# Splitting the bias product of a windowed attention into two half-width products, and moving one expert's matmul

## The chip, the cores and the metric

The kernel runs on one core of a Trainium2 chip. The metric is the device time of one execution in microseconds; a kernel's time is the median of its runs. The core has five engines, each with its own instruction stream: TensorE (PE in the profile: matmuls into PSUM; its weight loads have a row of their own, PEld), VectorE (DVE), ScalarE (ACT), GpSimd (POOL) and SyncE (SP), which here only issues DMAs. The engines wait for one another through semaphores. All data are 32-bit floats.

## The reference, cut to what matters

The input `x` is (2, 128, 256, 256). One layer adds a windowed attention and then a mixture of experts, each on a normalised input.

```python
# attention (b, 128 channels, 256 x 256), 4 heads of 32, 8x8 windows of queries, 12x12 of keys
qkv  = einsum('bchw,oc->bohw', layernorm_c(x), W_qkv)
attn = einsum('bnd,bmd->bnm', q * SCALE, k)
attn = attn + rel_pos_emb(q, rel_height, rel_width) + FIXED_MASK   # -inf off every second row, column
attn = softmax(attn)                                              # over the keys of one query
out  = einsum('bnm,bmd->bnd', attn, v)
x    = x + einsum('bchw,oc->bohw', out, W_out)
# experts: 8 experts of 128 -> 128, the best 2 of a token, weighted
t = layernorm_t(tokens(x))
p = softmax(t @ router_w + router_b);  top_p, top_i = top_k(p, 2);  top_p /= sum(top_p)
x = x + sum_k top_p[k] * (t @ expert_w[top_i[k]] + expert_b[top_i[k]])
```

`rel_pos_emb` is the sum of two terms: the query times the row of `rel_height` that belongs to the vertical distance between query and key, and the same with `rel_width` and the horizontal distance. Because of the mask a query only meets keys at an odd distance class, so that pixels of one parity of row and column form an attention of their own. A number added to all logits of one query does not change its softmax.

## The kernel before

A strip is 8 image rows; it falls into 4 *planes* by parity, so there are 2 x 32 x 4 = 256 planes of 4 x 128 = 512 queries. The main loop takes one plane per *stage*. While the attention of plane `n` runs, the projections of plane `n + 1` (`ahead`) are made, and the experts work on 512 tokens of an earlier strip. Generators are advanced step by step, and the order in which the loop advances them is the order of the instructions on every engine.

The projections of a plane, with `mm_tile` taking the next of three PSUM buffers that go round:

```python
def mm_tile(name):
    return ps_mm.tile([P, 512], F32, tag="mm", name=name)          # pool ps_mm: bufs=3

def project(n, state):
    ...
    values(0)                    # pvv: four 128x128 products, copied to vv by ACT
    yield
    pu = mm_tile(f"pu{n}")       # the bias product: 9 + 9 distances for each of 4 heads
    nc.tensor.matmul(pu, lhsT=wrel, rhs=inner, start=True, stop=True)
    uT = work.tile([P, PR, 4, 32], F32, tag="uT", name=f"uT{n}", bufs=1)
    nc.vector.transpose(uT, pu.rearrange("p (a m s) -> p a s m", a=PR, s=4))
    state["shift"] = lambda: shift(uT, n, state)
    yield
    ...                          # pk: keys, copied to kcol by ACT
    yield
    pq = mm_tile(f"pq{n}")
    nc.tensor.matmul(pq, lhsT=wq, rhs=inner, start=True, stop=True)
    ...                          # copied to qs by ACT
    yield
    values(4)
    yield
```

`shift` lays the distances out for the keys (two copies) and transposes them into `au`, from which the next stage's `scores` begins: 16 products with constant `keys` as weights put the bias into `att`, and 64 small ones add q times k.

The main loop, cut to the order of what the change touches (`ex` is the set of experts under way, `nxt` the one after it, `new` the one whose gates are being fetched):

```python
for n in range(n_planes + 7):
    ...
    next(score, None)            # bias products, first half of the scores
    ...                          # route(...): the gates of an earlier 512 tokens, on DVE
    next(score, None)            # second half of the scores; exp on ACT
    next(ahead, None)            # pvv, first half
    nxt.fetch(7, nc.scalar)
    ...                          # spread(...): transpose of the gates (gT), DMA to DRAM and back
    next(ahead, None)            # pu, and the transpose uT on DVE
    if n + 1 < n_planes:
        states[n + 1]["shift"]() # DVE
    next(ahead, None)            # pk
    next(ahead, None)            # pq
    for e in (4, 6, 7, 5):
        ex.product(e)
    ...
    next(norm, None)             # squares on ACT
    next(attn, None)             # row sums and first half of exp(scores) times v
    nxt.means()                  # DVE
    ...                          # nxt.times(0..4, 6): six products with the gates on DVE
    ex.end()                     # DVE: adds the experts' sum
    next(attn, None)             # second half; DVE: transpose of the sums, reciprocal
    next(attn, None)             # DVE: o
    ex = nxt
    next(norm, None)             # plt: sums for the norms
    ...
    next(ahead, None)            # pvv, second half
    ex.product(0)
    made = next(norm, None)      # DVE and ACT: 1 / deviation
    ex.product(1)
    ex.product(2)
    ...                          # POOL: times(5), ln1, times(7), columns
    next(outp, None)             # po: output product
    ex.product(3)
    next(outp, None)             # DVE: adds po to x
    ...
```

One `ex.product(e)` is a 128x128 by 128x512 product into a PSUM buffer of its own (`acc`).

Of the kernel before, what the change touches and what calls it, by code (L numbers as in the profile page):

```python
# [11 lines left out]
F32 = mybir.dt.float32  # L12
AF = mybir.ActivationFunctionType
ALU = mybir.AluOpType
# [3 lines left out]
P = 128  # L18
HEADS, DH = 4, 32
# [3 lines left out]
NEG = -1e30  # L23
# [16 lines left out]

R = 8
KR, KC = 6, 10
NK = KR * KC
SLOT = 64
BLOCK, FIRST_LIMIT = 256, 95
NU = 9


@with_exitstack
def kernel(
# [31 lines left out]
    work = ctx.enter_context(tc.tile_pool(name="work", bufs=2))  # L84
# [10 lines left out]
    def ctile(shape, name):  # L95
        return const.tile(shape, F32, tag=name, name=name)
# [24 lines left out]
    wall = ctile([P, 4, P], "wall")  # L121
# [51 lines left out]
    relT = []  # L173
    for rname, rsb in zip(("relh", "relw"), relsb):
        pr = mm_tile(f"p_{rname}")
# [5 lines left out]
        relT.append(rT)  # L181
    mid = n_rel // 2
    lo = mid - 2 * (PR - 1)
    relbd = ctile([P, P], "relbd")
    nc.gpsimd.memset(relbd, 0.0)
    for h in range(HEADS):
        hp = slice(h * DH, (h + 1) * DH)
        for j in range(2):
            c0 = h * DH + NU * j
            nc.vector.tensor_copy(  # L190
                relbd[hp, c0 : c0 + NU], relT[j][hp, lo : lo + 2 * NU - 1 : 2]
            )
    wrel = ctile([P, P], "wrel")
    pr = mm_tile("p_wrel")
    nc.tensor.matmul(pr[:, :P], lhsT=wall[:, 0, :], rhs=relbd, start=True, stop=True)
    nc.vector.tensor_copy(wrel, pr[:, :P])

    xn, xcol, kcol = [], [], []
    for i in range(2):
# [8 lines left out]
        nc.gpsimd.memset(kcol[i][:, NP - 1, KC - 1 : NK : KC], 0.0)  # L208


    auT = []
    for i in range(2):
        auT.append(ctile([P, PR, 4, 32], f"auT{i}"))
        nc.gpsimd.memset(auT[i], 0.0)
        nc.gpsimd.memset(auT[i][:, :, :, KR + 6 : KR + 7], NEG)


    def rstd(p4, k0, k1, name):
# [123 lines left out]

    def shift(uT, n, state):

        for j in range(2):
            shifted = uT[:, :, :, NU * j + 3 : NU * j + 9]
            dims = [list(d) for d in shifted.ap]
            dims[1 + j][0] -= 1
            nc.vector.tensor_copy(
                auT[n % 2][:, :, :, 6 * j : 6 * j + 6],  # L350
                bass.AP(shifted.tensor, shifted.offset, dims),
            )
        au = work.tile([P, 2 * NP, PR, 4], F32, tag="au", name=f"au{n}")
        nc.vector.transpose(au.rearrange("p m a s -> p a s m"), auT[n % 2])  # L354
        state["au"] = au

    def project(n, state):

        i, pl = divmod(n, 4)
        xp = xn[i % 2][:, pl // 2, pl % 2]  # L360
        inner = xp[:, 1 : 1 + PR, 1 : PC + 1]
        xl, kk = xcol[pl], kcol[pl]

        vv = work.tile([P, HP, P], F32, tag="vv", name=f"vv{n}")

        def values(t0):
            pv = mm_tile(f"pvv{n}_{t0}")
            for t in range(4):
                nc.tensor.matmul(  # L369
                    pv[:, t * P : (t + 1) * P],  # L370
                    lhsT=xl[:, t0 + t].rearrange("p a k -> p (a k)"),
                    rhs=wv,
                    start=True,
                    stop=True,
                )
            nc.scalar.copy(vv[:, t0 : t0 + 4, :].rearrange("p t c -> p (t c)"), pv)  # L376

        values(0)
        yield

        pu = mm_tile(f"pu{n}")
        nc.tensor.matmul(pu, lhsT=wrel, rhs=inner, start=True, stop=True)  # L384
        uT = work.tile([P, PR, 4, 32], F32, tag="uT", name=f"uT{n}", bufs=1)
        nc.vector.transpose(uT, pu.rearrange("p (a m s) -> p a s m", a=PR, s=4))  # L386
        state["shift"] = lambda: shift(uT, n, state)
        yield

        rows = list(ln_rows(i))  # L390
        for part in (rows[-4:], rows[:-4]):
            if not part:
                continue
            pk = mm_tile(f"pk{n}_{part[0]}")
            m = len(part)
            nc.tensor.matmul(  # L396
                pk[:, : m * PC],
                lhsT=wk,
                rhs=xp[:, part[0] : part[0] + m, 1 : PC + 1],
                start=True,  # L400
                stop=True,
            )
# [33 lines left out]
    def scores(n, state):  # L436


        qs, kk, au = state["qs"], state["kk"], state["au"]
        turn = place(n // 4, 0) // 2  # L440
        att = ps_att.tile([P, 4, 512], F32, tag="att", name=f"att{n}")
        sc = att[:, :, 0:HQ]
        for w in range(2):
            for half in range(2):
                rows = slice(half * SLOT, (half + 1) * SLOT)
                for h in range(HEADS):
                    hp = slice(h * DH, (h + 1) * DH)
                    nc.tensor.matmul(
                        sc[rows, h].rearrange("p (t w z) -> p t w z", w=2, z=16)[:, :, w],
                        lhsT=keys[hp, turn, w],  # L450
                        rhs=au[hp, half * NP + w : (half + 1) * NP : 2].rearrange(
                            "p t a s -> p t (a s)"
                        ),
                        start=(w == 0),
                        stop=False,
                    )
        for t in range(HP):
            if t == HP // 2:
                yield
            for half in range(2):  # L460
                rows = slice(half * SLOT, (half + 1) * SLOT)
                m0 = 2 * (half * HP + t)
                for h in range(HEADS):
                    hp = slice(h * DH, (h + 1) * DH)
                    nc.tensor.matmul(  # L465
                        sc[rows, h, 32 * t : 32 * t + 32],
                        lhsT=kk[hp, half * HP + t, :],
                        rhs=qs[hp, m0 : m0 + 2].rearrange("p m a s -> p (m a s)"),
                        start=False,
                        stop=(t == HP - 1),  # L470
                    )
# [257 lines left out]
    n_planes = 4 * len(strips)  # L729
# [19 lines left out]
    states = {0: {}}  # L749
    for _ in project(0, states[0]):  # L750
        pass
    states[0]["shift"]()
    if n_planes > 1:
        columns(1)

# [17 lines left out]
    gated, ex, nxt = None, NoExperts(), NoExperts()  # L773
# [4 lines left out]
    with tc.manual_schedule(engines={ET.PE, ET.DVE, ET.Activation, ET.Pool, ET.SP}):  # L778
        for n in range(n_planes + 7):
            i, pl = divmod(n, 4)  # L780
            score, attn, outp, ahead, norm, rout = none, none, none, none, none, none
# [44 lines left out]
            next(attn, None)  # L826
            nxt.means()
            new.fetch_means()
# [12 lines left out]
            ex = nxt  # L841
# [84 lines left out]
```

The softmax here doesn't subtract the row's maximum and nothing guards it: scores larger than these inputs give would overflow.

## Time and profile before

| | |
|---|---|
| time, median of 3 | 4486.36 us (4485.98 to 4488.05) |
| span of the profiled execution | 4480.1 us |
| DVE busy | 3996.2 us (89%) |
| ACT busy | 1467.7 us (33%) |
| POOL busy | 1317.7 us (29%) |
| mean TensorE clock granted | 0.997 of full speed |
| DMA | 828.12 MB, 185 GB/s on average |

A busy time is the time in which an engine had at least one instruction under way. Matmuls overlap, so a record of a matmul lasts longer than the step to the next one: times per product are therefore read as differences between starts in the timeline. A 32-bit product of 128x512 leaves two records. The row of the engine that is nearly always busy, and the timeline of one stage, are shown in the prediction, where they are read.

In the timeline a line is: start in us, length in us, engine, line of the program, operation, output<-inputs, shape, number of records merged, and in brackets the idle time before it and who ended it.

### The profile page before, as it was taken

How to read it: one execution, taken by the hardware profiler on the slowest of the kernel's cores; microseconds unless marked ns; L12 is line 12 of the kernel's file. 1: busy time of each engine (PE TensorE's matmuls, PEld its weight loads, DVE VectorE, ACT ScalarE, POOL GpSimd, SP SyncE). 2: the span in 40 equal slices, each digit the busy share in tenths (PEclk: the TensorE clock that was granted, in tenths of full speed). 3: DMA queues.
4: the chain of work that ended last, by engine and by line, in shares of the span. 5: the costliest groups of instructions: out<-in, count | busy, mean ns of one | idle time of the engine just before them, and what ended most of it. 6: DMA issues, size and time to landing. Idle time of an engine off the chain costs nothing. (4 is left out here: it accounts for less than half of the span.)

```text
span 4480.1 us, 224632 instructions
## 1 busy us (share of the span) xinstructions
PE 4422.6 (99%) x96321; PEld 2683.3 (60%) x96321; DVE 3996.2 (89%) x11850; ACT 1467.7 (33%) x4022; POOL 1317.7 (29%) x1815
## 2 busy tenths in 40 slices
PE   7999999999999999999999999999999999999997
PEld 5666666666666666666666666666666666666653
DVE  5899999999899999998989999999999999989887
ACT  3333333333333333333333333333333333333321
POOL 1232323232323233232323232323232323232321
PEclk9999999999999999999999999999999999999999
DMA  2565666566656666666666566666665666566655
GB/s 83 174 191 185 192 185 192 186 191 185 193 184 192 185 191 187 189 188 188 189 187 189 187 190 185 193 183 193 184 193 185 192 185 192 186 191 186 190 164 186
DMA packets 519284, 828.12 MB, mean 185 GB/s; under 512 B 124186, under 2 KB 125850, under 8 KB 518298
## 3 DMA queue, kind: packets, MB, share of 16 engines
q1 hardware_dynamic: 517568, 813.46, 58.3%
q8 instruction: 769, 12.60, 1.1%
q14 instruction: 217, 1.78, 0.2%
q10 hardware_dynamic: 730, 0.29, 0.0%
HBM read 737.95 MB, written 75.56 MB: 182 GB/s over the span
## 5 line engine op out<-in xcount | busy, mean ns | idle before, releaser
L686 PE MATMUL acc<-xe,ew 128*128 128x512 f32 x4096 | 1889.0, 594 | 19.6 <-DVE gb L660 18.8
L686 PEld LDWEIGHTS acc<-xe,ew 128*128 128x128 f32 x4096 | 758.8, 190 | 885.7 <-issue 861.8
L677 DVE TENSOR_TENSOR xe<-xs,gb 128x512 f32<-128x512 f32 x1536 | 950.9, 687 | 10.2 <-PE acc L686 0.7
L681 POOL COPY last<-xe 128x1 f32<-128x1 f32 x256 | 47.9, 187 | 3060.8 <-DVE gb L660 3054.6
L376 ACT COPY vv<-pvv 128x512 f32<-128x512 f32 x512 | 299.8, 586 | 1395.7 <-PE pvv L369 1379.6
L677 POOL TENSOR_TENSOR xe<-xs,gb 128x512 f32<-128x512 f32 x512 | 650.8, 1272 | 5.9 <-PE att L496 2.5
L369 PE MATMUL pvv<-wt,xcol 128*128 128x128 f32 x4096 | 594.3, 288 | 2.5 <-POOL xcol L331 1.5
L369 PEld LDWEIGHTS pvv<-wt,xcol 128*128 128x128 f32 x4096 | 496.4, 191 | 64.8 <-issue 51.8
L272 POOL TENSOR_TENSOR xn<-xt,rb 128x512 f32<-128x512 f32 x249 | 375.0, 1506 | 66.5 <-DMA rb<-gd 55.9
L465 PE MATMUL att<-qs,kcol 32*64 32x32 f32 x32768 | 392.4, 226 | 0.8 <-issue 0.7
L465 PEld LDWEIGHTS att<-qs,kcol 32*64 32x64 f32 x32768 | 391.0, 130 | 1.0 <-issue 1.0
L496 PEld LDWEIGHTS att<-pT,vv 64*32 64x32 f32 x32768 | 348.0, 105 | 39.4 <-issue 2.5
L496 PE MATMUL att<-pT,vv 64*32 64x32 f32 x32768 | 343.2, 200 | 2.3 <-issue 2.3
L473 ACT ACTIVATE pT<-att 128x1024 f32<-128x1024 f32 x256 | 261.9, 1023 | 243.1 <-PE att L465 239.7
L548 ACT ACTIVATE sq<-xt 128x512 f32<-128x512 f32 x505 | 292.7, 631 | 0.0
L354 DVE STREAM_TRANSPOSE au<-auT 128x512 f32<-128x512 f32 x256 | 269.2, 1052 | 9.0
L524 PE MATMUL po<-o,wt 128*128 128x512 f32 x512 | 262.0, 593 | 6.1 <-DVE o L516 3.2
L384 PE MATMUL pu<-xn,wrel 128*128 128x512 f32 x512 | 262.5, 594 | 0.0
L407 ACT COPY kcol<-pk 128x560 f32<-128x560 f32 (+2 forms) x344 | 174.1, 506 | 268.2 <-PE pk L396 265.3
L418 PE MATMUL pq<-xn,wt 128*128 128x512 f32 x512 | 262.0, 593 | 0.0
L396 PE MATMUL pk<-xn,wt 128*128 128x512 f32 (+2 forms) x528 | 261.0, 578 | 0.0
L386 DVE STREAM_TRANSPOSE uT<-pu 128x512 f32<-128x512 f32 x256 | 182.8, 714 | 78.0 <-PE pu L384 77.0
(2697 smaller groups left out, 5243.8 us busy)
## 6 DMA issues: line engine op xcount, KB each, us to landing
gb<-gd SPq DMA_DIRECT2D x2048, 256.0 KB, 4.0
xt<-in_x_dram SPq DMA_DIRECT2D x256, 256.0 KB, 4.9
sb<-gd SPq DMA_DIRECT2D x256, 256.0 KB, 3.5
out_dram<-xt SPq DMA_DIRECT2D x256, 256.0 KB, 4.2
rb<-gd SPq DMA_DIRECT2D x249, 256.0 KB, 3.3
gd<-gT SPq DMA_DIRECT2D x516, 16.0 KB, 3.0
ew<-in_L_ffn_expert_w_dram SPq DMA_DIRECT2D x1, 512.0 KB, 5.0
eb<-in_L_ffn_expert_b_dram SPq DMA_DIRECT2D x1, 512.0 KB, 5.7
```

Source lines behind the costliest of these rows:

```text
L272: eng.tensor_tensor(xn[i % 2][:, :, :, k, 1 : PC + 1], ln1_src(i, k).rearrange("p (y j x) -> p y x j", y=2, x=2), rb.rearrange("p (y j x) ...
L354: nc.vector.transpose(au.rearrange("p m a s -> p a s m"), auT[n % 2])
L369: nc.tensor.matmul(pv[:, t * P : (t + 1) * P], lhsT=xl[:, t0 + t].rearrange("p a k -> p (a k)"), rhs=wv, start=True, stop=True,)
L376: nc.scalar.copy(vv[:, t0 : t0 + 4, :].rearrange("p t c -> p (t c)"), pv)
L384: nc.tensor.matmul(pu, lhsT=wrel, rhs=inner, start=True, stop=True)
L418: nc.tensor.matmul(pq, lhsT=wq, rhs=inner, start=True, stop=True)
L465: nc.tensor.matmul(sc[rows, h, 32 * t : 32 * t + 32], lhsT=kk[hp, half * HP + t, :], rhs=qs[hp, m0 : m0 + 2].rearrange("p m a s -> p (m a ...
L496: nc.tensor.matmul(av[hp, half, 32 * t : 32 * t + 32], lhsT=vv[rows, t, hp], rhs=pT[rows, h, 32 * t : 32 * t + 32], start=True, stop=True,)
L524: nc.tensor.matmul(po, lhsT=wo, rhs=state["o"].rearrange("p f z -> p (f z)"), start=True, stop=True)
L548: nc.scalar.activation(sq, src, AF.Square)
L677: eng.tensor_tensor(self.xe[e], self.xs, self.gb.pop(e), ALU.mult)
L686: nc.tensor.matmul(self.acc, lhsT=ew[:, e, :], rhs=self.xe.pop(e), start=(e == 0), stop=not self.xe)
```

## The change

Three things are done together.

1. The bias product is halved. The value for the last distance is subtracted from the other eight when the weights `relbd` are built, once, so that 8 + 8 columns (`NB = 16`) per head are left instead of 9 + 9, and 64 weight columns for the four heads. The plane's 512 queries are cut into two halves of 256; both use the same 64 columns, one writes PSUM partitions 0 to 63 and the other 64 to 127. `pu` and `uT` have half the columns. `shift` needs four copies and two clearings for the layout, and its last transpose writes a tile `both` of half the size. In it the two halves stand on different partitions than the bias products want them, so a new step `send` moves them into a permanent `au` with eight small DMAs of 16 partitions x 1 KB each, issued from ACT.
2. The bias product stands directly behind the scores, ahead of the first half of `pvv`, and with it takes its PSUM buffer first.
3. `ex.product(3)`, which followed the output product `po`, is issued at the start of the next stage's group behind `pq`, ahead of experts 4, 6, 7 and 5.

`FIRST_LIMIT` (where the instruction stream of a stage is aligned) goes from 95 to 99, for the four instructions that the second half product adds.

```diff
-BLOCK, FIRST_LIMIT = 256, 95
+BLOCK, FIRST_LIMIT = 256, 99
 NU = 9
+NB = 16
@@ weights of the bias product @@
-            nc.vector.tensor_copy(
-                relbd[hp, c0 : c0 + NU], relT[j][hp, lo : lo + 2 * NU - 1 : 2]
+            c0 = h * NB + (NU - 1) * j
+            last_d = lo + 2 * (NU - 1)
+            nc.vector.tensor_tensor(
+                relbd[hp, c0 : c0 + NU - 1],
+                relT[j][hp, lo : last_d - 1 : 2],
+                relT[j][hp, last_d : last_d + 1].broadcast_to([DH, NU - 1]),
+                ALU.subtract,
             )
@@ shift @@
-        for j in range(2):
-            shifted = uT[:, :, :, NU * j + 3 : NU * j + 9]
             ...
-        au = work.tile([P, 2 * NP, PR, 4], F32, tag="au", name=f"au{n}")
-        nc.vector.transpose(au.rearrange("p m a s -> p a s m"), auT[n % 2])
+        for up, (rows, start) in enumerate(((slice(0, 64), 3), (slice(64, P), 1))):
             ...                                  # one copy each, on 64 partitions
+        for h in range(2):
             ...                                  # one copy each
+        nc.vector.memset(to[0:64, 0, :, :, 5:6], 0.0)
+        nc.vector.memset(to[:, :, 0, :, 11:12], 0.0)
+        both = work.tile([P, 2 * NP, 8], F32, tag="both", name=f"both{n}")
+        nc.vector.transpose(
+            both.rearrange("p m (a s) -> p a s m", a=2), to.rearrange("p a s h k -> p a s (h k)")
+        )
+    def send(n, state):
+        both = state.pop("both")
+        for up in range(2):
+            for h in range(HEADS):
+                r = (up * HEADS + h) * NB
+                nc.scalar.dma_start(au[n % 2][h * DH : h * DH + NB, up], both[r : r + NB])
@@ project @@
-        values(0)
-        yield
         pu = mm_tile(f"pu{n}")
-        nc.tensor.matmul(pu, lhsT=wrel, rhs=inner, start=True, stop=True)
-        uT = work.tile([P, PR, 4, 32], F32, tag="uT", name=f"uT{n}", bufs=1)
-        nc.vector.transpose(uT, pu.rearrange("p (a m s) -> p a s m", a=PR, s=4))
+        for up in range(2):
+            nc.tensor.matmul(
+                pu[up * 64 : (up + 1) * 64, 0 : NQ // 2],
+                lhsT=wrel,
+                rhs=inner[:, 2 * up : 2 * up + 2],
+                start=True,
+                stop=True,
+            )
+        uT = work.tile([P, 2, 4, 32], F32, tag="uT", name=f"uT{n}", bufs=1)
+        nc.vector.transpose(uT, pu[:, 0 : NQ // 2].rearrange("p (a m s) -> p a s m", a=2, s=4))
         state["shift"] = lambda: shift(uT, n, state)
         yield
+        values(0)
+        yield
@@ main loop @@
             next(score, None)
-            next(ahead, None)
             nxt.fetch(7, nc.scalar)
             ...
                 states[n + 1]["shift"]()
             next(ahead, None)
             next(ahead, None)
-            for e in (4, 6, 7, 5):
+            next(ahead, None)
+            for e in (3, 4, 6, 7, 5):
                 ex.product(e)
             ...
             next(norm, None)
+            if n + 1 < n_planes:
+                send(n + 1, states[n + 1])
             next(attn, None)
             ...
             next(outp, None)
-            ex.product(3)
             next(outp, None)
```

More of the change, by code (lines that the diff above doesn't have):

```diff
@@ L183 @@
     lo = mid - 2 * (PR - 1)
-    relbd = ctile([P, P], "relbd")
+    relbd = ctile([P, HEADS * NB], "relbd")
     nc.gpsimd.memset(relbd, 0.0)
@@ L188 @@
         for j in range(2):
-            c0 = h * DH + NU * j
-            nc.vector.tensor_copy(
-                relbd[hp, c0 : c0 + NU], relT[j][hp, lo : lo + 2 * NU - 1 : 2]
+            c0 = h * NB + (NU - 1) * j
[5 more added lines that the diff above has]
+                ALU.subtract,
             )
-    wrel = ctile([P, P], "wrel")
+    wrel = ctile([P, HEADS * NB], "wrel")
     pr = mm_tile("p_wrel")
-    nc.tensor.matmul(pr[:, :P], lhsT=wall[:, 0, :], rhs=relbd, start=True, stop=True)
-    nc.vector.tensor_copy(wrel, pr[:, :P])
+    nc.tensor.matmul(
+        pr[:, : HEADS * NB], lhsT=wall[:, 0, :], rhs=relbd, start=True, stop=True
+    )
+    nc.vector.tensor_copy(wrel, pr[:, : HEADS * NB])
     xn, xcol, kcol = [], [], []
@@ L208 @@
         nc.gpsimd.memset(kcol[i][:, NP - 1, KC - 1 : NK : KC], 0.0)
-    auT = []
+    auT, au = [], []
     for i in range(2):
-        auT.append(ctile([P, PR, 4, 32], f"auT{i}"))
+        auT.append(ctile([P, 2, 4, 2, NB], f"auT{i}"))
         nc.gpsimd.memset(auT[i], 0.0)
-        nc.gpsimd.memset(auT[i][:, :, :, KR + 6 : KR + 7], NEG)
+        nc.gpsimd.memset(auT[i][:, :, :, :, KR + 6 : KR + 7], NEG)
+        au.append(ctile([P, 2, 2 * NP, 8], f"au{i}"))
+        nc.gpsimd.memset(au[i], 0.0)
     def rstd(p4, k0, k1, name):
@@ L343, in shift @@
     def shift(uT, n, state):
-        for j in range(2):
-            shifted = uT[:, :, :, NU * j + 3 : NU * j + 9]
-            dims = [list(d) for d in shifted.ap]
-            dims[1 + j][0] -= 1
+        to = auT[n % 2]
+        for up, (rows, start) in enumerate(((slice(0, 64), 3), (slice(64, P), 1))):
+            src = uT[rows, :, :, start : start + 6]
+            step, block = src.ap[1][0], src.ap[2][0]
+            dims = [list(src.ap[0]), [step - 1, 2], [block // 2, 8], [1, 6]]
             nc.vector.tensor_copy(
-                auT[n % 2][:, :, :, 6 * j : 6 * j + 6],
-                bass.AP(shifted.tensor, shifted.offset, dims),
-            )
-        au = work.tile([P, 2 * NP, PR, 4], F32, tag="au", name=f"au{n}")
-        nc.vector.transpose(au.rearrange("p m a s -> p a s m"), auT[n % 2])
-        state["au"] = au
+                to[rows, :, :, :, 0:6].rearrange("p a s h k -> p a (s h) k"),
+                bass.AP(src.tensor, src.offset, dims),
+            )
+        src = uT[:, :, :, NU + 2 : NU + 8]
+        step, block = src.ap[1][0], src.ap[2][0]
+        for h in range(2):
+            dims = [list(src.ap[0]), [step, 2], [block - 1, 4], [1, 6]]
+            nc.vector.tensor_copy(
+                to[:, :, :, h, 6:12], bass.AP(src.tensor, src.offset + h * NB, dims)
+            )
[4 more added lines that the diff above has]
+            both.rearrange("p m (a s) -> p a s m", a=2), to.rearrange("p a s h k -> p a s (h k)")
+        )
+        state["both"] = both
+    def send(n, state):
[4 more added lines that the diff above has]
+                nc.scalar.dma_start(au[n % 2][h * DH : h * DH + NB, up], both[r : r + NB])
     def project(n, state):
@@ L376, in values @@
             nc.scalar.copy(vv[:, t0 : t0 + 4, :].rearrange("p t c -> p (t c)"), pv)
-        values(0)
-        yield
-        pu = mm_tile(f"pu{n}")
-        nc.tensor.matmul(pu, lhsT=wrel, rhs=inner, start=True, stop=True)
-        uT = work.tile([P, PR, 4, 32], F32, tag="uT", name=f"uT{n}", bufs=1)
-        nc.vector.transpose(uT, pu.rearrange("p (a m s) -> p a s m", a=PR, s=4))
-        state["shift"] = lambda: shift(uT, n, state)
+        pu = mm_tile(f"pu{n}")
+        for up in range(2):
+            nc.tensor.matmul(
+                pu[up * 64 : (up + 1) * 64, 0 : NQ // 2],
[3 more added lines that the diff above has]
+                stop=True,
+            )
+        uT = work.tile([P, 2, 4, 32], F32, tag="uT", name=f"uT{n}", bufs=1)
+        nc.vector.transpose(uT, pu[:, 0 : NQ // 2].rearrange("p (a m s) -> p a s m", a=2, s=4))
+        state["shift"] = lambda: shift(uT, n, state)
+        yield
+        values(0)
         yield
@@ L436, in scores @@
     def scores(n, state):
-        qs, kk, au = state["qs"], state["kk"], state["au"]
+        qs, kk, bias = state["qs"], state["kk"], au[n % 2]
         turn = place(n // 4, 0) // 2
@@ L448, in scores @@
                     nc.tensor.matmul(
-                        sc[rows, h].rearrange("p (t w z) -> p t w z", w=2, z=16)[:, :, w],
+                        sc[rows, h].rearrange("p (t w a z) -> p t w a z", w=2, a=2, z=8)[:, :, w],
                         lhsT=keys[hp, turn, w],
-                        rhs=au[hp, half * NP + w : (half + 1) * NP : 2].rearrange(
-                            "p t a s -> p t (a s)"
+                        rhs=bias[hp, :, half * NP + w : (half + 1) * NP : 2].rearrange(
+                            "p a t z -> p t a z"
                         ),
@@ L752 @@
     states[0]["shift"]()
+    send(0, states[0])
     if n_planes > 1:
```

## The prediction

> **What bounds the kernel now.** I read the page's row of engines first, then the busy times over a long stretch, then the timeline of one stage on TensorE (PE) and the same on VectorE (DVE), and last the list of waits.
>
> ```profile
> PE 4422.6 (99%) x96321; PEld 2683.3 (60%) x96321; DVE 3996.2 (89%) x11850; ACT 1467.7 (33%) x4022; POOL 1317.7 (29%) x1815
> ```
>
> PE is busy all the time, and from 2000 to 2800 us it is busy for 799.99 of 800 us. DVE has 723.38 us there, 90%, so it is a close second. Busy alone does not prove that PE is the bound, since matmuls overlap; what proves it is that the starts on PE follow each other without a hole. One stage:
>
> ```profile
> 2001.45 0.69 PE L448 MATMUL att<-au,keys 32*64 32x128 f32 x32
> 2001.93 1.53 PE L465 MATMUL att<-qs,kcol 32*64 32x32 f32 x128
> 2003.39 1.16 PE L369 MATMUL pvv<-wt,xcol 128*128 128x128 f32 x8
> 2004.39 1.02 PE L384 MATMUL pu<-xn,wrel 128*128 128x512 f32 x2
> 2005.25 1.02 PE L396 MATMUL pk<-xn,wt 128*128 128x512 f32 x2
> 2006.11 1.02 PE L418 MATMUL pq<-xn,wt 128*128 128x512 f32 x2
> 2006.97 3.59 PE L686 MATMUL acc<-xe,ew 128*128 128x512 f32 x8
> 2010.49 0.66 PE L486 MATMUL att<-pT,ones 64*32 64x256 f32 x16
> ...
> 2012.22 0.43 PE L554 MATMUL plt<-xt,rw 128*32 128x128 f32 x8
> 2012.46 0.40 PE L554 MATMUL plt<-sq,rw 128*32 128x128 f32 x8
> 2012.68 0.40 PE L554 MATMUL plt<-xt,rw 128*32 128x128 f32 x8
> 2012.90 0.40 PE L554 MATMUL plt<-sq,rw 128*32 128x128 f32 x8
> 2013.23 1.16 PE L369 MATMUL pvv<-wt,xcol 128*128 128x128 f32 x8
> 2014.22 2.74 PE L686 MATMUL acc<-xe,ew 128*128 128x512 f32 x6
> 2016.80 1.02 PE L524 MATMUL po<-o,wt 128*128 128x512 f32 x2
> 2017.66 1.02 PE L686 MATMUL acc<-xe,ew 128*128 128x512 f32 x2
> 2018.61 0.69 PE L448 MATMUL att<-au,keys 32*64 32x128 f32 x32
> ```
>
> From bias product to bias product (L448) the stage takes 2018.61 - 2001.45 = 17.16 us. Every step between two starts can be read as a price: a product of 128x512 costs 0.86 (pu L384 to pk L396 to pq L418); four of them behind pq 3.52; bias 0.48; scores 1.46; half of pvv 1.00. The prices fill the stage, and nothing waits. DVE at the end of this stage and in the next:
>
> ```profile
> 2017.86 0.69 DVE L529 TENSOR_TENSOR xt<-po,xt 128x512 f32<-128x512 f32 x1
> ...
> 2022.09 0.24 DVE L625 STREAM_TRANSPOSE gT<-g 128x64 f32<-128x64 f32 x1
> 2022.61 0.72 DVE L386 STREAM_TRANSPOSE uT<-pu 128x512 f32<-128x512 f32 x1 [0.28 <-PE pu L384]
> 2023.36 0.33 DVE L349 COPY auT<-uT 128x96 f32<-128x96 f32 x2
> 2023.73 1.06 DVE L354 STREAM_TRANSPOSE au<-auT 128x512 f32<-128x512 f32 x1
> ```
>
> L529 adds the output product po to x. It starts 1.06 us after po's start on PE (2016.80), that is, as soon as po's records end (2016.80 + 1.02). Then DVE works without a pause through the routing until gT (L625) ends at 2022.33, and only there stands a hole: 0.28 us until pu is done. So DVE runs only just ahead of PE, and **its order is fixed: po's addition, routing, gT, uT**. The list of waits says the same for the whole run: uT waited for pu 186 times, 77.0 us in all, and the addition for po 11 times only, 3.5 us.
>
> **What the Trainium skill says.** (1) "Perfetto Trace Analysis", its opening note: matmul busy time is a bad measure, because matmuls are pipelined. The trace agrees (a record of 1.02 us with a step of 0.86), so I count in steps. (2) "TensorE: Matmul & The Clock Gate", "Part 3: Packing small matmuls": products in different column groups of the array run at the same time. The trace agrees: each of the four plt groups (L554) is four products with 32 weight columns each, on four column groups, and a group costs 0.22 us to 0.24 us, a quarter of the 1.00 us of the four full-width products of pvv. (3) The same page, Part 1: ScalarE and VectorE are strict FIFO, and on PE only weight loads are pulled ahead, matmuls stay in order. So a matmul that waits for a late DVE instruction holds up everything behind it. Nothing in this trace contradicts that; the wait itself is not yet in it.
>
> **The change part by part.**
>
> *The halved product.* It removes one product of 0.86. It adds two of 256 columns in two column groups; by (2) they should take the time of one, half of 0.86 = 0.43, plus one more change of the array's shape, for which the step from the last plt group to pvv, 0.33 instead of 0.22, gives 0.11. Sum 0.54, saving 0.32 per stage. If PE stayed dense, the stage would be 17.16 - 0.32 = **16.84 us**.
>
> *DVE's layout work.* Before: from uT to the next product L671 2024.63 - 2022.61 = 2.02 us. After: uT on half the columns, for which I interpolate between 128x128 (L563, 0.33) and 128x512 (0.72): 0.46; two copies of 96 elements at 0.17 per step, two of 48 at some 0.13, two clearings, and a last transpose of about half of L354's 1.05. Together about 1.7. DVE gains some 0.3 us; this is beside the path unless DVE is the bound.
>
> *The eight DMAs.* They leave ACT behind its squares. In the changed program some of them wait for slots that the gate transfers rb and sb have to free first. Before, sb landed some 8 us after gT's end (issued 4.56 after it, 3.5 to landing); with some 3 us more (the 16 KB gd writes take 3.0) the table is there 11 us after gT, while the next bias product comes about 13 us after it (see below). I take this as **hidden, with some 2 us to spare**.
>
> *Moving expert 3, and pu ahead of pvv.* This is what decides, and it removes no work. Two things happen.
>
> First, the buffers. mm tiles go round in three PSUM buffers. Before, the order was pvv, pu, pk, pq, so pq took the buffer of pvv, which ACT empties early (in the program before, pq waits for ACT's copy L376). After, the order is pu, pvv, pk, pq: **pq takes the buffer of pu and must wait until DVE has read it in uT**. In the changed program the wait in front of pq is indeed on DVE's uT.
>
> Second, the time of uT. It is tied to po by DVE's order: po's start + 1.06 to the addition, + 2022.33 - 2017.86 = 4.47 to the end of gT, + 0.46 for uT, + 0.04 to hand over (pu's end 2022.57 to uT's start 2022.61) = po + 6.03. And PE reaches pq sooner, since expert 3 no longer stands between po and the bias: 0.95 from po to the bias (the step 2017.66 to 2018.61, product and change of shape), 0.48, 1.46, 0.54 for pu, 1.00 for pvv, 0.86 for pk = po + 5.29. Before, PE got there at po + 0.86 + 0.95 + 4.66 = po + 6.47 and had no such wait. So **PE stands still for 0.74 us in front of pq**.
>
> The whole ring, as a check: from pq's start to po's start PE takes 2016.80 - 2006.11 = 10.69 before, and with expert 3 in it 11.55. Add po to pq, 6.03: **17.58 us per stage**, of which PE fills 16.84. PE must start again with a cold pipeline; some part of a weight load (0.19) may not be hidden: I add 0.06, 17.64. This is 0.48 more than before. Expert 3 is on the ring because it now stands between pq and po, while in its old place it lay beside the DVE's routing.
>
> Experts and projections are both there from stage 7 to 254, so 248 times: 248 x 0.48 = 119 us; the seven stages ahead of that gain some 2 us in all. 4486.4 + 119 - 2 = **about 4603 us**.
>
> **The rivals.**
>
> *PE stays dense (16.84).* Then 248 x 0.32 = 79 us are saved, 4405 us. For it: PE is the bound, and the halved product is cheaper by a mechanism that the trace shows. Against it: it needs uT to be done at po + 5.29, and DVE has 4.47 us of routing alone ahead of it. It would hold if DVE's order were another or the ring had a fourth buffer.
>
> *DVE becomes the bound.* In a stage of 17.16 DVE waits 0.28 for pu; without that and with 0.3 less layout work it needs about 16.6. Against it also: the sums' transpose L506 could start 6.7 after uT, but it needs the end of the product of weights and v, some 7.6 after uT's start, so DVE idles there. DVE counts as part of the ring, not as the bound.
>
> *The table comes late.* Then PE waits in front of the bias product. For it: a chain of three DMAs and an ACT engine that stands in line behind them. Against it: the 2 us to spare; and a delay of up to 0.74 would only take the place of the wait at pq. If it were 1 us late beyond that, the stage would be 18.6 us and the time near 4840.
>
> *GpSimd and DVE in each other's way.* Some DVE instructions are long because GpSimd is busy (L229 has a median near 0.82 but 0.16 in the first stages). With sT later, L229 may meet shorter GpSimd instructions. That would gain nothing, as DVE then waits for po.
>
> **Range and chances.** The ring is a sum of measured steps; open are uT's length, the restart, and the hand-over, together perhaps 0.15 to either side, so 0.32 to 0.63 per stage: 4566 to 4643, which I widen a little to **4560 to 4640**. 2% is 89.7 us, that is 0.36 per stage, at the lower end of this. Slower by over 2%: 0.79. Within 2%: 0.16, for a wait of half the size. Faster by over 2%: 0.05; even the dense rival gives only 1.8%.
>
> **What the changed profile would show.** Waits of PE (or PEld) at pq for DVE's uT, some 0.7 us each, near 180 us in all, and PE busy down to about 95%; no wait of uT for pu any more; DVE waiting some 0.9 us for PE at the transpose of the sums and some 0.7 us at po's addition; the pair of half products with a step near 0.5 us; no wait at the bias product; a stage of about 17.6 us. The prediction is wrong if pq starts without a hole (then 16.84 per stage and some 4405), if the half products do not overlap (this would shift the hole, not the stage), or if the bias product waits for a DMA.

## The result, and the profile after

The changed kernel takes **4683.0 us** (median of 4 runs, 4676.21 to 4694.24) against 4487.2 us before: ratio **1.0438, interval 1.0413 to 1.0463**. The prediction was 4603 us, with a range up to 4640. The direction was right, the size was not: 196 us were lost instead of 117.

The page of the changed kernel, row of engines and DMA queues (queue: packets, MB, share of 16 engines):

```profile
PE 4509.8 (96%) x96833; PEld 2685.1 (57%) x96833; DVE 3775.4 (80%) x12874; ACT 1494.5 (32%) x4022; POOL 1321.5 (28%) x1817
...
q10 hardware_dynamic: 66266, 33.97, 2.7%
```

PE fell from 99% to 96% busy: it stands still now. Queue q10 is the one that ACT issues to; it had 730 packets and 0.29 MB before, and the eight DMAs per plane are nearly all of what it moves now. Queue q8, whose kind is "instruction", has 769 packets and 12.60 MB in both kernels: 16.4 KB each, and about three go by per stage.

The list of waits of the changed kernel (engine, tile and line, what it waited for: us in total, times, longest):

```profile
DVE sT L547 <- PE att L537: 303.4, 255, 5.3
PEld pq L459 <- DVE uT L424: 262.1, 237, 1.3
...
PE pq L459 <- DVE uT L424: 78.4, 192, 0.6
...
PEld att L489 <- DMA au<-both: 71.9, 84, 2.1
...
PE pq L459 <- issue: 28.2, 43, 1.7
...
PE att L489 <- DMA au<-both: 11.8, 29, 1.3
```

A wait can stand there twice, for the weight loads (PEld) and for the matmuls (PE), so the two rows of one wait are not to be added; only PE's is time in which no matmul ran. The predicted wait is there (pq for uT, 192 to 237 times) and so is its consequence on DVE, which now waits for PE at sT, the transpose of the sums. Two lines were not predicted: the bias product (L489) waits for its table, and pq waits for "issue", which is time in which PE waited for nothing that the profile shows. Two stages of PE's timeline, one clean and one not:

```profile
2016.97 1.02 PE L565 MATMUL po<-o,wt 128*128 128x512 f32 x2
2017.92 0.69 PE L489 MATMUL att<-au,keys 32*64 32x128 f32 x32
...
2021.44 1.02 PE L437 MATMUL pk<-xn,wt 128*128 128x512 f32 x2
2022.88 1.13 PE L459 MATMUL pq<-xn,wt 128*128 128x512 f32 x2 [0.41 <-DVE uT L424]
...
2028.69 1.34 PE L537 MATMUL att<-pT,vv 64*32 64x32 f32 x128
...
2034.54 1.02 PE L565 MATMUL po<-o,wt 128*128 128x512 f32 x2
2036.21 1.20 PE L489 MATMUL att<-au,keys 32*64 32x128 f32 x27 [0.65 <-DMA au<-both]
...
2042.64 0.70 PE L459 MATMUL pq<-xn,wt 128*128 128x512 f32 x1 [0.91 <-issue]
...
2048.02 1.50 PE L537 MATMUL att<-pT,vv 64*32 64x32 f32 x128
```

The clean stage runs from po to po in 2034.54 - 2016.97 = 17.57 us, and that is the predicted ring (po, DVE's addition and routing, uT, pq, the experts, po again: 17.58). The next po comes at 2054.03, 19.49 us later. That stage shows all three troubles: a **late table** (the bias starts 1.67 us behind po instead of 0.95), a **hole inside pq** (its second record comes after 0.91 us of idle time with no releaser), and a **stretched product of weights and v** (L537, below called av: 1.50 us instead of 1.34). In the middle of the run (some 230 stages) the mean stage is 17.94 us, a quarter of the stages have 17.57 or less, and nearly all of the excess lies in these three places.

In the description of the change one thing is to be corrected: `FIRST_LIMIT` counts the instructions of a stage ahead of the first boundary, and the four that were added there are waits ahead of the first four bias products, each of which now waits for two DMAs; the second half product lies behind that point.

### The profile page after: what moved, and what is told of

The parts are those of the page before. It is cut to its first block, busy times and chain, and to the rows that moved or that the text cites. A ratio compares the mean times of both kernels' runs of the same rounds, so it can differ in the third digit from the quotient of the medians.

```text
span 4692.4 us, 228272 instructions
## 1 busy us (share of the span) xinstructions
PE 4509.8 (96%) x96833; PEld 2685.1 (57%) x96833; DVE 3775.4 (80%) x12874; ACT 1494.5 (32%) x4022; POOL 1321.5 (28%) x1817
## 3 DMA queue, kind: packets, MB, share of 16 engines
q8 instruction: 769, 12.60, 1.1%
## 5 line engine op out<-in xcount | busy, mean ns | idle before, releaser
L727 PE MATMUL acc<-xe,ew 128*128 128x512 f32 x4096 | 1849.2, 594 | 18.6 <-DVE gb L701 17.8
L118 ACT COPY xt<-onesm 128x1 f32<-128x1 f32 x247 | 47.3, 191 | 1483.3 <-DMA au<-both 1032.7
L547 DVE STREAM_TRANSPOSE sT<-att 128x512 f32<-128x512 f32 x256 | 183.5, 717 | 303.4 <-PE att L537 303.4
L537 PEld LDWEIGHTS att<-pT,vv 64*32 64x32 f32 x32768 | 376.3, 105 | 49.1 <-issue 1.9
L459 PE MATMUL pq<-xn,wt 128*128 128x512 f32 x512 | 300.3, 651 | 107.7 <-DVE uT L424 78.4
L537 PE MATMUL att<-pT,vv 64*32 64x32 f32 x32768 | 381.6, 200 | 1.8 <-issue 1.7
L570 DVE TENSOR_TENSOR xt<-po,xt 128x512 f32<-128x512 f32 x256 | 177.2, 692 | 138.2 <-PE po L565 138.1
L459 PEld LDWEIGHTS pq<-xn,wt 128*128 128x128 f32 x512 | 85.9, 189 | 338.3 <-DVE uT L424 262.1
L489 PEld LDWEIGHTS att<-au,keys 32*64 32x64 f32 x8192 | 146.7, 131 | 221.8 <-issue 147.0
L633 ACT ACTIVATE lg<-lg 128x32 f32<-128x32 f32 x256 | 58.7, 229 | 671.3 <-DVE lg L632 671.3
```

Source lines behind the costliest of these rows:

```text
L537: nc.tensor.matmul(av[hp, half, 32 * t : 32 * t + 32], lhsT=vv[rows, t, hp], rhs=pT[rows, h, 32 * t : 32 * t + 32], start=True, stop=True,)
L547: nc.vector.transpose(sT, av[:, 2:4])
L570: nc.vector.tensor_add(xv, po.rearrange("p (m a s) -> p m a s", a=PR, s=4), xv)
L727: nc.tensor.matmul(self.acc, lhsT=ew[:, e, :], rhs=self.xe.pop(e), start=(e == 0), stop=not self.xe)
```

## The experiments

Three questions: is the ring as predicted, where do the other 95 us come from, and is there a version without either? In each table PE's stages are those of the middle of the run, times in us, read as differences of starts.

### Undoing one move, or doing the moves alone

*Bias product behind the first half of pvv again:*

```diff
-        pu = mm_tile(f"pu{n}")      # ... both halves, uT, yield
         values(0)
         yield
+        pu = mm_tile(f"pu{n}")      # ... both halves, uT, yield
```

> The changed kernel with one part undone: the halved bias product stands behind the first half of pvv again, so that pq takes the PSUM buffer of pvv and not that of the bias product. Expert 3 stays ahead of the four, the eight small DMAs stay. Theory A (ring: pq waits for VectorE's transpose uT because it takes pu's buffer): the 0.6 us wait in front of pq goes, a stage without other waits falls from 17.57 to about 16.9 us, and the whole from 4683 to about 4480 to 4530 us, the rest over 4410 being late tables and holes in the instruction stream. Theory B (the small DMAs and what they hold up cost all of it): about 4650 to 4700 us.

*Expert 3 behind po again:*

```diff
-            for e in (3, 4, 6, 7, 5):
+            for e in (4, 6, 7, 5):
@@
             next(outp, None)
+            ex.product(3)
```

> The changed kernel with the other move undone: expert 3 follows the output product again, the halved bias product stays directly behind the scores and pq still takes its buffer. Theory A: the ring of pq, po, routing and uT is shorter by one product of 0.86 (17.57 becomes 16.7), less than TensorE's own 16.84, so the wait at pq goes here too and the whole is about 4480 to 4530 us. Theory B: about 4650 to 4700 us. A third view, that the order pu, pvv alone makes pq wait wherever expert 3 stands: about 4600 us.

*The kernel before with both moves, and nothing of the halved product or its DMAs:*

> The kernel before with the two moves alone: the full bias product goes directly behind the scores and expert 3 ahead of the four; no halving and no small DMAs. Theory A: pq waits for uT, which is 0.3 us longer than in the changed kernel, so a stage takes about 17.85 us instead of 17.16 and the whole about 4650 us. Theory B: as the kernel before, 4487 us.

*The changed kernel without the eight DMAs (the bias is left out of the logits, its product and layout are still made):*

```diff
-BLOCK, FIRST_LIMIT = 256, 99
+BLOCK, FIRST_LIMIT = 256, 95
@@
-            if n + 1 < n_planes:
-                send(n + 1, states[n + 1])
```

> The changed kernel without its eight small DMAs per stage: the bias products read a table that stays zero, so that the bias is left out of the result; all products, copies and transposes are still made, and the instruction stream is aligned as before (95), as four waits are gone. Theory A with nothing else: every stage at the ring's 17.57 us, the whole about 4590 us. If the holes in TensorE's instruction stream (in the product of weights and v, and behind pq) come from the pauses at pq and not from the small DMAs, they stay and the whole is about 4660 us. Theory B: about 4410 us.

| | time | ratio to before, interval | shortest / mean stage |
|---|---|---|---|
| pu back | 4641.73 | 1.0349 [1.0334, 1.0365] | 16.87 / 17.73 |
| expert 3 back | 4589.42 | 1.0232 [1.0213, 1.0251] | 16.89 / 17.49 |
| moves only | 4651.73 | 1.0375 [1.0358, 1.0392] | 17.83 / 17.84 |
| no DMAs | 4586.37 | 1.0226 [1.0211, 1.0242] | 17.56 / 17.59 |

Where no DMA disturbs it, the ring is all there is. With the moves alone eight of ten stages have 17.83 to 17.84 us, and without the DMAs 17.56 to 17.63. The lists of waits of these two, moves only and then no DMAs:

```profile
PE pq L418 <- DVE uT L381: 98.4, 238, 1.2
```

```profile
PE pq L459 <- DVE uT L424: 101.1, 236, 1.7
```

So **the ring costs 4586.4 - 4485.3 = 101 us** net of what the halved product saves, and the eight DMAs cost the rest. Undoing either move breaks the ring: a quarter of the stages with pu back have 17.09 us or less, and a tenth of those with expert 3 back 16.90. But the time does not come down to the 4480 to 4530 us that were expected of both, because the other troubles grow. With pu back, the table is later still (bias to scores 0.685 us in the mean instead of 0.487). With expert 3 back no table is late any more, but in 86 of 229 stages the second record of pq comes over 0.9 us behind the first instead of 0.43 (pq to the row sums 4.86 instead of 4.39 in the mean):

```profile
PE pq L459 <- issue: 60.2, 136, 1.4
```

### What of the DMAs costs time: their waits or their traffic

*The same DMAs into a tile that nobody reads (bias left out; boundaries at 95, as without the DMAs):*

```diff
-                nc.scalar.dma_start(au[n % 2][h * DH : h * DH + NB, up], both[r : r + NB])
+                nc.scalar.dma_start(spare[n % 2][h * DH : h * DH + NB, up], both[r : r + NB])
```

> The changed kernel with its eight small DMAs per stage sent to a spare tile that nobody reads; the bias products read a table that stays zero (the bias is left out of the result). The traffic and the standing in line on ScalarE are all there, but TensorE waits for none of these DMAs; aligned as before (95). Theory W (the holes in TensorE's instruction stream come from TensorE's sequencer standing at the waits for the tables, so that it loses its lead over the array): every stage at 17.57 us, the whole about 4590 us as without the DMAs. Theory F (the small DMAs themselves hold up the fetching of instructions): holes in the product of weights and v and behind pq stay, the whole about 4640 to 4670 us.

*The bias products read the table of the plane before, which has long landed (the logits get that plane's bias):*

```diff
-        qs, kk, bias = state["qs"], state["kk"], au[n % 2]
+        qs, kk, bias = state["qs"], state["kk"], au[(n + 1) % 2]
```

> The changed kernel, but the bias products of a plane read the table of the plane before it (the bias in the result is that of another plane). The DMAs, their number and the four extra waits in front of the bias products are as in the changed kernel; only the data waited for landed a whole stage earlier. Theory W: no late table and no holes, about 4590 us. Theory F: the late tables go, the holes stay: about 4650 to 4670 us. A third view, that the four extra wait instructions alone cost it: as changed, about 4680 us.

Measured: 4659.39 (1.0382 [1.0366, 1.0397]) and 4660.70 (1.0383 [1.0368, 1.0399]). In both PE does not wait for a table, and the holes in pq and the stretched av stay. The DMAs cost 4659.4 - 4586.4 = **73 us without PE waiting for them**; the late tables add 4683.0 - 4660.7 = **22 us**. 101 + 73 + 22 = 196. By the stages of the run with the spare tile, some 39 of the 73 us lie in av (row sums to plt 1.88 us in the mean instead of 1.72 without the DMAs, times 248 stages) and some 19 in pq (pq to the row sums 5.44 instead of 5.36). The theory that extra waits in the instruction stream did it has fallen.

### Who issues the DMAs

Expert 3 is back behind po in both, so that the ring is out of the way.

```diff
-                nc.scalar.dma_start(au[n % 2][h * DH : h * DH + NB, up], both[r : r + NB])
+                nc.sync.dma_start(...)      # and ahead of rb, the next gates
+                nc.gpsimd.dma_start(...)    # the other run
```

> Expert 3 follows the output product again, and the eight small DMAs are issued from SyncE as soon as VectorE has the table, between the writing of the gates and the reading back of their row rb, which follows after them. So they no longer wait behind the gate transfers, and the table lands some 5 us earlier. Everything is computed. Theory A with W: no wait at pq, no late table, no holes; a stage takes the 16.90 us of the undisturbed stages of the run with expert 3 put back, the whole 4487 - 248 x 0.26 = about 4425 us. Theory F: holes stay, about 4500 to 4560 us.

> As with expert 3 put back behind the output product, but the eight small DMAs are issued from GpSimd, which idles at that time, so that they wait for no other transfer's slot and hold up no work of ScalarE. Everything is computed. Theory A with W: as above, about 4425 us, unless GpSimd's own issuing is slow and holds up its products for experts 5 and 7. Theory F: about 4500 to 4560 us.

From SP it took 4947.11 us (1.1019 [1.1003, 1.1036]), a miss. The timeline of SP suggests why:

```profile
2013.32 5.07 SPq L389 DMA_DIRECT2D au<-both  x8
```

Eight issues take 5.07 us here (5.69 in the median stage) and push the gates' broadcast rb back by as much; GpSimd waited for it 240 times, 1008.3 us in all. That this is the whole loss was not tested: the hole in pq is there too, and av is stretched in 211 of 215 stages. From GpSimd it took 4567.15 us (1.0171 [1.0154, 1.0188]). The hole in pq stayed (95 of 229 stages), **but av was not stretched once**. The two holes are thus different things.

### The hole in pq: an instruction packet

In the trace, every late second record of pq (over 0.9 us behind the first) comes 1.2 to 1.6 us after a packet of queue q8 ends: in 32 of 32 stages of the changed kernel and in 86 of 86 with expert 3 back. Smaller delays look the same: from 0.6 us on there are 46 and 170 such records, 45 and 170 of them at this distance. The program aligns its stream so that boundaries of 256 instructions lie at 99, 355 and 611 in each stage, and 355 falls inside pq. The packet in question ends 4.09 us behind po without the DMAs (4.97 in one of ten stages), and 4.45 (5.86) with them, while pq's second record, behind the wait for uT, is due at 5.91 + 0.53 = 6.44. With 1.4 us from packet to matmul, the first fits (4.97 + 1.4 = 6.37) and the second (5.86 + 1.4 = 7.26) does not.

With expert 3 back the hole is not shown to be the DMAs' doing. There the packet ends 3.79 us behind the start of the bias product (4.22 in one of ten stages), and in the kernel before, which sends none, 3.81 (4.19). What differs is what stands at the boundary: pq's second record is due 4.40 + 0.43 = 4.83 us behind the bias, ahead of 3.79 + 1.4. In the kernel before, by the count of records, the boundary at 351 lies just behind pq, in the first expert's product, which is due at 5.52. A run with expert 3 back and no DMAs was not made.

If that is so, shifting the boundaries must move the hole. One number, in three kernels, and a third position in a fourth:

```diff
-BLOCK, FIRST_LIMIT = 256, 99
+BLOCK, FIRST_LIMIT = 256, 131      # and 170
```

> The changed kernel with one number altered: the padding of the instruction stream puts the boundaries of the fetched 16 KB instruction packets at records 131, 387 and 643 of a stage instead of 99, 355 and 611. Theory F (the eight DMAs delay instruction packets, and TensorE stops at the boundary whose packet is late): the hole inside pq goes, because the boundary now lies in the row sums behind the experts; the hole in the product of weights and v moves from about record 100 to about record 117 or shrinks. About 0.16 us of the 0.37 us per stage go, 4683 - 40 = about 4640. The late tables stay (about 0.065 per stage). Rival (the holes have nothing to do with the position of the boundary): pq keeps its late second record in some 30 of 230 stages as before, time stays at 4683.

> Expert 3 back behind po, and the same shift of the boundaries. Theory F: without it the stage had 17.49 us in the mean against a shortest of 16.9, with pq to row sums at 4.86 instead of 4.39; that excess goes, mean stage about 17.05, time about 4470, for the first time no slower than the kernel before (4487). Rival: unchanged, 4589.

> As the kernel with expert 3 back and 131, with the boundaries at 170, 426 and 682: the second early in the product of weights and v, the third in the sums for the norms. Theory F: any hole lies at the start of the product of weights and v now and none in pq; between 4450 and 4540. Rival: unchanged, 4589.

> Expert 3 back, the eight DMAs issued from GpSimd, boundaries at 131. Theory F: 4567 (its time with 99) less the hole in pq, about 4450 to 4480. Rival: unchanged, 4567.

| | time | ratio to before, interval | pq over 0.9 us behind, stages | av stretched, stages |
|---|---|---|---|---|
| changed kernel (99, ACT) | 4683.0 | 1.0438 [1.0413, 1.0463] | 32 of 223 | 122 of 223 |
| the same, 131 | 4665.82 | 1.0408 [1.0392, 1.0423] | 0 of 224 | 199 of 224 |
| expert 3 back (99, ACT) | 4589.42 | 1.0232 [1.0213, 1.0251] | 86 of 229 | 110 of 228 |
| expert 3 back, 131 | **4442.57** | **0.9908 [0.9893, 0.9923]** | 0 of 236 | 18 of 236 |
| expert 3 back, GpSimd | 4567.15 | 1.0171 [1.0154, 1.0188] | 95 of 229 | 0 of 229 |
| expert 3 back, GpSimd, 131 | 4478.69 | 0.9988 [0.9980, 0.9996] | 1 | 0 |
| expert 3 back, 170 | 5443.75 | 1.2141 [1.2122, 1.2160] | 0 of 191 | 5 of 191 |

At 131 the hole in pq is gone but for one stage, and one number in a stream of 96,833 matmuls took 147 us off the kernel with expert 3 back. The changed kernel gained only 17 us and stayed 26 over what was expected, since its av got worse. The position 170 was expected between 4450 and 4540 and missed by far, but in the way the theory says. Its timeline on PE:

```profile
2009.15 0.38 PE L595 MATMUL plt<-sq,rw 128*32 128x128 f32 x2
2012.89 0.43 PE L595 MATMUL plt<-sq,rw 128*32 128x128 f32 x3 [3.36 <-issue]
```

The third boundary, 682, now lies in plt, and PE stops there, behind the tenth record, in 187 of 191 stages and for 2.66 us (median). It goes on 1.38 us after a packet's end (1.26 to 1.51 in eight of ten stages), the same distance as in pq. What I had not seen is that this packet itself ends 14.03 us behind po (median) instead of 9.5 with 131. What starts a fetch was not tried. Not all of the 854 us over the same kernel with 99 are these holes: after them PE is granted less of its clock (0.933 in the mean instead of 0.994; half of it in 168 stretches, most of them 3.4 us long).

The Trainium skill, "Runtime: NRT & Kernel Launch", section "Instruction fetch mechanics", says that instructions are fetched in 16 KiB blocks of 256 and that the cost of a boundary is mostly hidden. The first agrees with the 16.4 KB per packet here. The second held for the kernel before (nine of ten stages 17.16 to 17.17) and not for these: a late record of pq comes 1.25 us behind the first instead of 0.53 (median of those over 0.9 in the changed kernel), and the stop in plt has 2.66 us.

### The stretched av: an issue on ACT or SP

Shifting the boundary did not mend av; with 131 and the moves kept it was stretched in more stages, not fewer. Single records show stalls of 0.1 to 0.2 us, one or two per stage, and their ends stand at a fixed distance from the issues of the eight DMAs. From the timeline of the changed kernel with 131, ACT's issues in two short windows, and PE's av from the end of the stall that follows each:

```profile
1229.94 0.60 ACTq L389 DMA_DIRECT2D au<-both  x1
...
1230.58 0.61 ACTq L389 DMA_DIRECT2D au<-both  x1
```

```profile
1230.29 0.66 PE L537 MATMUL att<-pT,vv 64*32 64x32 f32 x50
...
1230.93 0.54 PE L537 MATMUL att<-pT,vv 64*32 64x32 f32 x35
```

The records next ahead start at 1230.15 and 1230.76, where the usual step is 0.008. So each stall ends 0.35 us after an issue began (1229.94, 1230.58). Of the 177 stalls in the changed kernel the middle half ends 0.35 to 0.36 us after one, and of 271 issues that began from 0.5 us ahead of av to 0.6 us before its end 226 were followed by a stall within 1 us. SP is like ACT: where it issues, 418 of 450 were, and the stalls end 0.34 us after the issue began. Where GpSimd issues, 1017 issues fell into the same stretch in three kernels and 1 was followed by a stall; where nothing is sent, there is none. That an issue of these DMAs on ACT or SP causes it is thus shown; by what path is open. Not every issue does: without the eight DMAs, 459 issues of the gates' broadcasts gb from SP fell into av, and no stall followed. With expert 3 back and 131 only 34 issues fall into that stretch, which is why 18 stages are all that is left.

### Closing the account

*The changed kernel, both moves kept, issued from GpSimd, 131:*

> The changed kernel with both moves kept, the eight DMAs issued from GpSimd instead of ScalarE, boundaries at 131. Theory (three separate costs of the DMAs: late table, instruction packet late in pq, stalls that follow an issue on ScalarE): the pq hole and the stalls in the product of weights and v are gone, the ring of 17.57 us stays, and perhaps some late tables; time 4590 to 4620, as the kernel without DMAs (4586) plus little. Rival (the traffic itself slows TensorE, whoever issues it): 4640 to 4666, as with ScalarE.

4630.27 us (1.0321 [1.0305, 1.0336]), 10 us over the range that was expected. The median stage has 17.59 us, pq is late once, av is never stretched and PE waits for a table 6 times. But 15 stages, about every 15th, are 1.5 to 4.1 us longer, 37 us together. Just ahead of each of them one DVE instruction is long (1.40 to 3.67 us). DVE's timeline at one:

```profile
2441.31 3.32 DVE L242 TENSOR_TENSOR u__136_46074<-r__136_46075 128x8 f32<-128x8 f32 x1
```

A DVE instruction of 128x8 elements takes 3.32 us instead of 0.17, while GpSimd works through two of its own (xn from 2441.38 and xe to 2444.09). The Trainium skill ("SBUF — State Buffer", "Summary: rules for kernel authors") says that of a DVE instruction with two SBUF inputs and a GpSimd one that reads SBUF, the second to issue waits until the first has finished. The trace fits only in part: here the DVE instruction outlasts two of GpSimd's that began after it. I did not test it apart, nor why it is every 15th stage. With expert 3 back, GpSimd and 131 there are 15 such stages too, 47 us together, which is more than the 36 us by which that kernel lies above the one with ACT. Less the 15 stages here, the time is 4630 - 37 = 4593, by the kernel without DMAs (4586) and by the prediction (4603). **Without the three costs the prediction would have stood.**

*Two controls for the best version: the kernel before with 131, and the halved product without either move (pu behind pvv, expert 3 behind po) with 131:*

> The kernel before with the boundaries moved from 95 to 131 and nothing else. Theory: it has no hole at a boundary (every stage 17.16 to 17.17), so nothing changes, 4480 to 4495. Rival: the alignment itself is worth something, and the 0.9% that e3_back_align131 gained over the kernel before is partly due to it: below 4465.

> Halved product and its DMAs, with the bias product behind the first half of pvv again and expert 3 behind po again, boundaries at 131. As TensorE is the bound there and the order alone differs, dense stages of about 16.9 us as in e3_back_align131, 4435 to 4450; the table is 1 us later. Rival (the bias product must go early, since uT and the layout come later on VectorE otherwise and the tables late): 4460 or more, with waits in front of the bias products.

The first took 4480.88 (0.9988 [0.9979, 0.9997]), so the alignment gives the kernel before next to nothing. The second took 4541.63 (1.0120 [1.0103, 1.0136]), a miss of 90 us. Its av is stretched again (row sums to plt 1.89 us instead of 1.72, 242 issues in the stretch named above), and from bias to pq it takes 4.58 instead of 4.39: the step from pvv to pu is 1.09 instead of 1.00 and that from pk to pq 0.96 instead of 0.86. Late tables, the rival's reason, are not seen (bias to scores 0.51 in the mean instead of 0.49). So the bias product does belong behind the scores, for another reason than was thought. From PE's timeline of the best version, expert 3 back and 131:

```profile
2016.60 1.02 PE L437 MATMUL pk<-xn,wt 128*128 128x512 f32 x2
2017.46 1.02 PE L459 MATMUL pq<-xn,wt 128*128 128x512 f32 x2
2018.32 3.59 PE L727 MATMUL acc<-xe,ew 128*128 128x512 f32 x8
```

pq follows pk by 0.86 and the experts follow pq by 0.86: PE has no wait for uT and no late packet. PE is dense again, 99% busy, at 16.89 us per stage (median; mean 16.94). This version has the whole computation and is 0.9% faster than the kernel before.

## Why the prediction was right or wrong

**Right: the ring, step by step.** "pq takes the buffer of pu and must wait until DVE has read it in uT", and "17.58 us per stage", 17.64 with the restart, was measured as 17.57. Inside it two errors partly cancelled. pq starts 5.91 behind po instead of 6.03: uT took 0.41 us instead of 0.46, and started 0.07 ahead of gT's end. The other part was 11.66 instead of 11.61, since the restart costs 0.10 (pq to the experts 0.96 or 0.97 instead of 0.86) and not 0.06. DVE in the clean stage:

```profile
2022.25 0.24 DVE L666 STREAM_TRANSPOSE gT<-g 128x64 f32<-128x64 f32 x1
2022.42 0.41 DVE L424 STREAM_TRANSPOSE uT<-pu 128x256 f32<-128x256 f32 x1
```

"PE stands still for 0.74 us" was 1.44 - 0.86 = 0.58. The layout took 1.84 us from uT to the next product (which starts at 2024.26) instead of 1.7; it lies beside the path, as was said.

**Nearly right: the halved product.** The pair has a step of 0.58 instead of 0.54, and the dense stage 16.89 instead of 16.84. That the two halves run together in two column groups holds.

**Wrong: "The eight DMAs ... hidden, with some 2 us to spare".** This step cost 95 us where it said 0, and "if the bias product waits for a DMA" was one of the prediction's own signs of being wrong. It asked only when the table would land, and even that was too early. The timeline of ACT behind the clean stage:

```profile
2026.22 6.37 ACTq L389 DMA_DIRECT2D au<-both  x6
```

The last issue ends 10.1 us after gT's end (2022.49), not some 8 us, as it would have to for a table at 11, and the next bias product goes ahead 13.7 us after it, 0.7 us later than due. "No wait at the bias product" was wrong with it. The reason given beside it, that such a delay would mostly take the place of the wait at pq, was right: in the middle of the run pu starts late in 55 of 227 stages, by 34 us together, and of these pq's start keeps 13. But the late stages also have the hole in pq more often (second record over 0.6 us behind the first in 37 of the 55, in 9 of the other 172), so that the 22 us are not the wait alone.

The larger part of the step, 73 us, was not in the sum at all: the DMAs slow PE without its waiting for them, by delaying instruction packets (shown for the changed kernel, not for the one with expert 3 back) and by their issue. No rival named it. The range was drawn from the uncertainty of the ring, and that uncertainty was indeed small; it held nothing for a cost that I had put at zero.

**The rivals.** PE stays dense: it needs expert 3 back in its old place, and got there at 16.89 us. DVE as the bound: no; it idles 0.84 us at sT in the clean stage. The late table: real, in about every fourth stage, and about as dear (22 us) as the hole in pq (some 19). GpSimd and DVE in each other's way: the instruction named there, L229, has 0.83 us in the median before and, as L242, 0.23 in the changed kernel, which gained nothing, as was said; it grew to over 2 us, in the middle of the run, only where GpSimd issues the DMAs.

**The purpose of the change.** Of its three parts, the halved product saves 0.28 us per stage, and the early place of the bias product is needed for it. Expert 3's move costs the most (with boundaries at 131 and issues on ACT 4665.8 - 4442.6 = 223 us), since it puts 0.86 us on a ring that had room for it between po and the bias.

## What to carry to other kernels

Moving a product without changing the work can create a ring through a rotating buffer and another engine's fixed order; add up that ring before and after, it comes out to a tenth of a microsecond. A small DMA is not free when it is early enough: look where its issue falls beside dense small matmuls, and whether instruction packets still come in time at the boundaries of the stream. When a stall has no releaser in the profile ("issue") and always stands at the same instruction, shift the stream by some instructions ahead of any other experiment; here one position was worth 147 us and another cost 854.

## What the runs showed of the hardware that was not expected

- PE stops at a boundary of its instruction stream when the 16 KB packet is late, and goes on 1.2 to 1.6 us after the packet's end, in pq (median 1.4) as in plt (1.38).
- An issue of one of the eight DMAs on ACT or SP is followed by a stall of 0.1 to 0.2 us in PE's 64x32 products that ends 0.34 to 0.36 us after the issue begins (226 of 271, 418 of 450); issues on GpSimd are not (1 of 1017).
- Eight issues of 16 KB take 5.69 us on SP (median, pauses included) and 3.88 us on GpSimd, about 0.5 each.
